# Softmax sums of the last attention unit: four key tiles summed on VectorE, two partial sums per group on TensorE

## The chip, the cores and the metric

The kernel runs on one core of one Trainium2 chip. The metric is the device time of one execution in microseconds (us), given as the median of several runs. The engines of the core have their own instruction queues and meet at semaphores: TensorE (PE in the profile, its weight loads PEld), VectorE (DVE), ScalarE (ACT), GpSimd (POOL) and SyncE (SP), whose queue issues nearly all of the transfers here.

## The reference

A decoder block on `x` of 4 x 1024 x 512 in float32: gated self-attention, cross-attention to a context of 4 x 1024 x 384, and a small feed-forward network, each behind a layer norm and added to its input. The change is in the cross-attention, which is, cut to what matters:

```python
q = (query @ Wq + bq).reshape(B, Nq, H, D).transpose(0, 2, 1, 3)    # B = 4, Nq = 1024, H = 16, D = 32
k = (key_value @ Wk + bk).reshape(B, Nkv, H, D).transpose(0, 2, 1, 3)
v = (key_value @ Wv + bv).reshape(B, Nkv, H, D).transpose(0, 2, 1, 3)
attn = jnp.einsum('bhqd,bhkd->bhqk', q, k) * scale
attn = jnp.clip(attn, -CLAMP, CLAMP)
attn = jax.nn.softmax(attn, axis=-1)
...
x = jnp.einsum('bhqk,bhkd->bqhd', attn, v).reshape(B, Nq, Cq)
return x @ Wo + bo
```

The softmax needs, for each head and query, the sum of the exponentials over all 1024 keys. How this sum is formed for the last batch element is what changes.

## The kernel before, in words

`moderate_path` does all of the work. It goes through eight **units**: `order` lists phase 0 (self-attention) and then phase 1 (cross-attention), each for the batch elements 0 to 3. The last unit, number 7, is the cross-attention of batch element 3. A unit has two halves of 512 queries (`hf`), a half has four **groups** of four heads (`g`), and a group has eight **key tiles** of 128 keys (`kt`). One call of `step(g, kt)` (L684) handles one key tile of one group, so that a unit has 64 steps.

The order of instructions is written out by hand; the instructions of each engine run in the order in which the code issues them. One step issues, in this order:

1. what `after(...)` has put on the list as due and not "behind" (`issue_due(False)`): the divisions of earlier groups;
2. `scores`: TensorE multiplies keys and queries into two PSUM tiles `s` (i = 0 for heads 0 and 1 of the group, i = 1 for heads 2 and 3; tag `s` has two buffers, L570), ScalarE takes the exponential of each into a tile `e` of 128 x 1024 (six buffers, L578 and L579), and VectorE adds `e` to running sums `es` (L585 for the first two key tiles, L587 after that);
3. what is due and "behind" (`issue_due(True)`): the closing sums of the group before (`add_up`);
4. `finish` of the step before: `times` multiplies the exponentials by the values into `av` (L601), and after the last key tile `normalize` copies `av` (L618) and has `add_up` come one step later.

Beside the steps, `run` (L933) spreads other work over them, the "items": projections (L87), layer norm, its transposes, the hidden units of the feed-forward network (ScalarE L862, VectorE L868). In the last unit these are, in each half: rest of the hidden units of an earlier half, the output projection of the half before (L87, L770, L774, L775), the feed-forward output (L879, L885), the layer norm with its way through memory (`root` L290 to L299, `norm` L303, the writing `away` L307, the reading `back` L312, the 32 x 32 block transposes L318), the input of the feed-forward network (`inputs`, L841) and then hidden units again.

**The sums before.** In units 4 to 6 (`shared` is false) VectorE adds all four heads, 14 additions of 128 x 1024 in a group, and `add_up` sums over the 128 partitions with four TensorE products with a column of ones (L631). In the last unit `shared` is true: VectorE adds only heads 0 and 1 (seven additions in a group). For heads 2 and 3 TensorE multiplies each `e` by the ones itself: at every second key tile `times` issues four such products, two key tiles by two heads (L609). `normalize` then copies that result too (L620), `add_up` issues two products for heads 0 and 1 (L631) and copies them (L632), and four small transfers bring both parts into one tile, in which `divide` adds them (L637, L642, L643, L647, L655). `divide` takes the reciprocal (L668), writes it to memory (L671) and reads it back spread over the partitions (L675); `multiply` uses it (L681).

The very last group, (unit 7, second half, group 3), is `closing`: it already has all four heads added on VectorE, and its final sums are taken by `settle` (L705) at the end, with ones repeated 32 times so that the result stands on all rows at once (L713). The code after the units (from L1045 on) finishes it: `divide` of `settle` in four pieces (L719, L720), the last projection, layer norm, transposes and feed-forward network.

All working tiles in SBUF come from pools with a fixed number of buffers for each tag. The transposed keys have the tag `k` with two buffers (L455); the last unit's keys are in one of them, and no unit after it needs the other.

Of the kernel before, what the change touches and what calls it, by code (L numbers as in the profile page):

```python
# [10 lines left out]
F32 = mybir.dt.float32  # L11
U32 = mybir.dt.uint32
AF = mybir.ActivationFunctionType
ALU = mybir.AluOpType
AX = mybir.AxisListType

P = 128
B, T, D = 4, 1024, 512
H, DH = 16, 32
NPR = H // 2  # L20
HG = 4
NT = T // P
NC = D // P
# [40 lines left out]
def moderate_path(tc: tile.TileContext, a: dict, out: bass.AP, flag: bass.AP):  # L64
    nc = tc.nc
    x = a["x"]
    with ExitStack() as st:
# [8 lines left out]
        p2 = enter(tc.tile_pool(name="mp2", bufs=2))  # L76
# [29 lines left out]
        ones = const.tile([P, 1], F32, name="ones")  # L106
# [158 lines left out]
        sm = pa.tile([P, HALF], F32, tag="sm", name="sm")  # L265
# [70 lines left out]
        order = [(ph, b) for ph in range(2) for b in range(B)]  # L336
# [5 lines left out]
        def after(steps, f, behind=False):  # L342

            soon.append((tick[0] + steps, behind, f))
# [206 lines left out]
        def attention(u, hf):  # L551

            ph, b = order[u]
            me = S[u]
            steps = []
            sums = 2 if ph == 0 else 1

            shared = ph == 0 or u + 1 == len(order)

            def apart(g):  # L560
                return 2 if u + 1 < len(order) else 3

            def closing(g):
                return (u, hf, g) == (len(order) - 1, 1, HG - 1)

            def scores(g, kt):
                q, k = me["q", hf], me["k"]
                es = []
                for i in range(2):
                    s = ps.tile([P, 2, HALF], F32, tag="s", name="s")  # L570
                    for j in range(2):
                        r = slice((2 * i + j) * DH, (2 * i + j + 1) * DH)
                        for m in range(0, P, 64):
                            nc.tensor.matmul(  # L574
                                s[m : m + 64, j, :], lhsT=k[r, g, kt * P + m : kt * P + m + 64], rhs=q[r, g, :],
                                start=True, stop=True,
                            )
                    e = p4.tile([P, 2, HALF], F32, tag="e", name="e", bufs=6)  # L578
                    nc.scalar.activation(e, s, AF.Exp, scale=SCALE)  # L579
                    es.append(e)  # L580
                me["e", kt] = es
                for i in range(1 if shared and not closing(g) else 2):
                    if kt == 1:
                        me.setdefault("es", {})[i] = p1.tile([P, 2, HALF], F32, tag=f"es{i}", name="es")
                        nc.vector.tensor_tensor(me["es"][i], me["e", 0][i], es[i], ALU.add)  # L585
                    elif kt > 1:
                        nc.vector.tensor_tensor(me["es"][i], me["es"][i], es[i], ALU.add)  # L587
                if ph == 0 and kt > 0:
                    if kt == 1:
                        me["eg"] = p1.tile([P, 2, HALF], F32, tag="es1", name="eg")  # L590
                    for h in range(2):
                        eg, gate = me["eg"][:, h, :], lambda t: me["sw"][:, t, HG * g + h, 1:2]
                        if kt == 1:
                            nc.vector.tensor_scalar(eg, me["e", 0][0][:, h, :], gate(0), None, ALU.mult)
                        nc.vector.scalar_tensor_tensor(eg, es[0][:, h, :], gate(kt), eg, ALU.mult, ALU.add)  # L595
                return es

            def times(g, kt, es):
                for h in range(HG):
                    r = slice(h * DH, (h + 1) * DH)  # L600
                    nc.tensor.matmul(  # L601
                        av[r, :], lhsT=me["v"][:, kt, HG * g + h, :], rhs=es[h // 2][:, h % 2, :],
                        start=(kt == 0), stop=(kt == NT - 1),
                    )
                if shared and kt % 2 and not closing(g):

                    for j in range(4):
                        t, h = kt - 1 + j // 2, j % 2
                        nc.tensor.matmul(  # L609
                            sm[j * DH : j * DH + sums, :],  # L610
                            lhsT=me["sw"][:, t, HG * g + 2 + h, :] if ph == 0 else ones, rhs=me["e", t][1][:, h, :],
                            start=(kt == 1), stop=(kt == NT - 1),
                        )

            def normalize(g):
                i = (u * 2 + hf) * HG + g
                both = p1.tile([P, 3, HALF], F32, tag="both", name="both")
                nc.scalar.copy(both[:, 0, :], av)  # L618
                if shared:
                    nc.scalar.copy(both[:, 1, :], sm)  # L620
                    added = [me["es"][0][:, 0, :], me["es"][0][:, 1, :]]
                    if ph == 0:
                        added += [me["eg"][:, 0, :], me["eg"][:, 1, :]]
                else:
                    added = [me["es"][h // 2][:, h % 2, :] for h in range(HG)]
                after(1, lambda: add_up(g, i, both, added), behind=True)

            def add_up(g, i, both, added):

                for j, e in enumerate(added):  # L630
                    nc.tensor.matmul(sm[j * DH : j * DH + 1, :], lhsT=ones, rhs=e, start=True, stop=True)  # L631
                nc.scalar.copy(both[:, 2, :], sm)  # L632

                c, s1, s2 = cs_[i % 2], sum1_d[i % 4], sum2_d[i % 4]
                rows = both.rearrange("(j r) s q -> j r s q", r=DH)
                n = len(added)
                nc.sync.dma_start(s1[0:n], rows[0:n, 0, 2, :])  # L637
                if not shared:
                    nc.sync.dma_start(c[:, 0, 0, :], s1[0:n].rearrange("h (q e) -> (h q) e", e=INNER))
                else:  # L640
                    for k in range(sums):
                        nc.sync.dma_start(s2[k], rows[:, k, 1, :])  # L642
                    nc.sync.dma_start(  # L643
                        c[0:64, 0:sums, 0, :], s1[0:n].rearrange("(s h) (q e) -> (h q) s e", h=2, e=INNER)
                    )
                    for k in range(sums):
                        nc.sync.dma_start(  # L647
                            c[64:, k, :, :], s2[k].rearrange("(p h) (q e) -> (h q) p e", h=2, e=INNER)
                        )
                after(apart(g), lambda: divide(g, i, both, c))  # L650
# [44 lines left out]
            def finish(g, kt, es):  # L695
                times(g, kt, es)
                if kt == NT - 1 and not closing(g):
                    normalize(g)
# [6 lines left out]
        def settle(u, hf, g):  # L705

            me = S[u]
            i = (u * 2 + hf) * HG + g
            rec = p1.tile([P, HALF], F32, tag="recb", name="recb")

            def sums():
                for j in range(HG):
                    nc.tensor.matmul(  # L713
                        sm[j * DH : (j + 1) * DH, :], lhsT=ones.to_broadcast([P, DH]), rhs=me["es"][j // 2][:, j % 2, :],
                        start=True, stop=True,
                    )

            def divide(t):
                nc.vector.reciprocal(rec[:, ts(t, P)], sm[:, ts(t, P)])  # L719
                nc.vector.tensor_tensor(me["q", hf][:, g, ts(t, P)], av[:, ts(t, P)], rec[:, ts(t, P)], ALU.mult)  # L720

            def look():
                nc.vector.tensor_reduce(marks[:, i : i + 1], sm, AX.X, ALU.add)
                nc.vector.tensor_reduce(marks[:, NS + i : NS + i + 1], rec, AX.X, ALU.add)

            return sums, divide, look
# [225 lines left out]
        def one(f):  # L952
            return [[(0, f)]]
# [4 lines left out]
        def ahead(u, what):  # L958

            return one(lambda: pres[u]["load"](what))  # L960
# [62 lines left out]
        p = pres[0]  # L1023
# [8 lines left out]
        first = p["x"][0] + one(warm) + p["ln"][0] + p["x"][1] + one(load_gates) + ahead(0, "q") + ahead(0, "v")  # L1032
# [7 lines left out]
        for u in range(n):  # L1040
            if u == 0:
                crossing.append(True)
            for hf in range(2):
                run(attention(u, hf), beside(u, hf))
# [9 lines left out]
        h = [part for item in held[0]["h"] for part in item]  # L1054
# [18 lines left out]
        h = sum(tail["h"], [])  # L1073
# [650 lines left out]
```

## Time and profile before

| what | value |
|---|---|
| time, median of 3 runs | 2200.52 us (2198.43 to 2201.12) |
| the profiled execution, first to last instruction | 2198.2 us |
| mean granted TensorE clock of that execution | 0.997 |
| first scores of the last unit | 1927.81 us after the start |
| first scores of the last unit's second half | 2036.25 us |
| last key tile's scores | 2141.55 us |
| from there to the end | 56.7 us |
| VectorE busy in all, additions L587 among it | 1562.5 us, 642.2 us |
| ScalarE busy in all, exponentials L579 among it | 1237.6 us, 993.4 us |

Times in the profile count from the first instruction of the profiled execution. "Line engine op out<-in xcount | busy us, mean ns" is a group of instructions that come from one line. The count is of the hardware's records: in float32 a product has two. The granted clock is the share of full speed at which the TensorE array was allowed to run. The chain of waits follows back from the last instruction, at each step to what released it; "idle before, releaser" is the engine's idle time and what ended it.

The work of each engine in the last unit, by stretches (the columns are: stretch, its length, then busy time and count of PE, PEld, DVE, ACT and POOL, the granted clock, the DMA engines' share and GB/s):

```profile
1927.81:1954.20 26.39, 26.15 (x260) 5.71 (x256) 14.37 (x21) 21.31 (x28) 0.00 (x0) 1.00 0.06 13
1954.20:1980.14 25.94, 25.94 (x273) 6.40 (x269) 14.55 (x27) 16.61 (x22) 0.00 (x0) 1.00 0.06 13
1980.14:2014.10 33.96, 33.70 (x328) 7.52 (x328) 25.61 (x47) 23.45 (x26) 0.19 (x1) 1.00 0.39 103
2014.10:2054.30 40.20, 39.60 (x404) 8.84 (x398) 19.94 (x33) 33.16 (x46) 0.00 (x0) 1.00 0.30 94
2054.30:2089.50 35.20, 35.20 (x357) 8.62 (x357) 17.09 (x26) 19.18 (x23) 0.00 (x0) 1.00 0.04 11
2089.50:2124.20 34.70, 34.33 (x332) 7.58 (x328) 25.61 (x46) 23.92 (x27) 0.19 (x1) 1.00 0.46 131
```

The first line is the first group of the unit; the third and the sixth are the stretches with the layer norm and its transposes, up to the input product of the feed-forward network (L841).

### The profile page before, as it was taken

To read this page: it belongs to the slowest core of one execution; us is meant where nothing else is said; L and a number is where in the kernel's file an instruction comes from. 1 tells how busy PE (TensorE), PEld (TensorE's weight loads), DVE (VectorE), ACT (ScalarE), POOL (GpSimd) and SP (SyncE) were. 2 spreads that over 40 slices of the span, in tenths; PEclk is the share of its full clock that TensorE was granted. 3 is DMA by queue.
4 is the path that set the end of the run, shared out by engine and by line. 5 is a ranking of instruction groups with operands and counts; after the bars stand their busy time and mean duration, and the time that the engine had idled before them with its cause. 6 is when DMAs were issued, how large, how long until landed. Compare 5 with 4: busy or idle time off the path is not lost.

```text
span 2198.2 us, 52765 instructions
## 1 busy us (share of the span) xinstructions
PE 2170.0 (99%) x22606; PEld 551.7 (25%) x22606; DVE 1562.5 (71%) x2526; ACT 1237.6 (56%) x1489; POOL 82.2 (4%) x118
## 2 busy tenths in 40 slices
PE   8999999999999999999999999999999999999996
PEld 3322222222222222222222222222222222222223
DVE  4478675796757957567677676877777777856477
ACT  0155545555455554555656566675757666577673
POOL 1000000030210000000000000000000000000000
PEclk9999999999999999999999999999999999999998
DMA  4412123132231221211222132222234142213131
GB/s 141 131 61 55 63 96 106 29 88 66 97 104 31 82 69 47 68 57 42 70 85 90 45 89 69 79 70 59 69 84 112 46 107 69 61 39 80 59 89 41
DMA packets 153304, 161.70 MB, mean 74 GB/s; under 512 B 46202, under 2 KB 91898, under 8 KB 151908
## 3 DMA queue, kind: packets, MB, share of 16 engines
q1 hardware_dynamic: 149068, 156.14, 24.6%
q8 instruction: 179, 2.93, 0.6%
q0 software_dynamic: 2144, 0.98, 0.3%
q10 hardware_dynamic: 1848, 1.12, 0.2%
q14 instruction: 65, 0.53, 0.1%
HBM read 115.40 MB, written 42.74 MB: 72 GB/s over the span
## 4 chain that ended last, share of the span: by engine, by line
PE 93%; DVE 3%; DMA 1%; ACT 1%; issue 1%; SPq 0%; DVEq 0%; ACTq 0%
PE f L87 36%; PE s L574 25%; PE av L601 21%; PE sm L609 6%; PE sm L631 3%; ACT e L579 1%; DMA w<-in_attn_Wo 1%; PE f L841 1%; PE f L879 1%; DVE g L868 1%; DVE es L587 1%; DMA rows_d<-r 0%; PE s L879 0%; PE f L471 0%; DMA rec_d<-rec 0%
## 5 line engine op out<-in xcount | busy, mean ns | idle before, releaser
L579 ACT ACTIVATE e<-s 128x1024 f32<-128x1024 f32 x1024 | 993.4, 1022 | 709.9 <-PE s L574 512.9
L587 DVE TENSOR_TENSOR es<-es,e 128x1024 f32<-128x1024 f32 x534 | 642.2, 1227 | 253.6 <-ACT e L579 251.6
L574 PE MATMUL s<-q,k 32*64 32x512 f32 x8192 | 607.5, 613 | 2.2 <-ACT e L579 0.5
L601 PE MATMUL av<-e,v 128*32 128x512 f32 x4096 | 550.4, 603 | 0.0
L87 PE MATMUL f<-xT,w 128*32 128x512 f32 x2816 | 333.7, 592 | 0.6 <-PE f L87 0.6
L595 DVE SCALAR_TENSOR_TENSOR eg<-e,sw,eg 128x512 f32<-128x512 f32 x448 | 318.5, 746 | 2.3
L585 DVE TENSOR_TENSOR es<-e 128x1024 f32<-128x1024 f32 x89 | 106.7, 1223 | 216.4 <-ACT e L579 185.4
L574 PEld LDWEIGHTS s<-q,k 32*64 32x64 f32 x8192 | 132.9, 130 | 445.6 <-ACT e L579 242.2
L87 PE MATMUL f<-w,q 128*32 128x512 f32 x1984 | 240.3, 593 | 0.0
L601 PEld LDWEIGHTS av<-e,v 128*32 128x32 f32 x4096 | 88.2, 108 | 403.7 <-issue 401.2
L87 PEld LDWEIGHTS f<-xT,w 128*32 128x32 f32 x2816 | 92.3, 110 | 211.0 <-issue 204.2
L609 PE MATMUL sm<-e,sw 128*2 128x512 f32 x1024 | 133.3, 592 | 0.0
L87 PE MATMUL f<-w,xT 128*32 128x512 f32 x896 | 106.0, 592 | 0.6 <-DVE q L284 0.6
L87 PEld LDWEIGHTS f<-w,q 128*32 128x32 f32 x1984 | 65.8, 110 | 148.9 <-issue 141.5
L87 PE MATMUL f<-w,ctxT 128*32 128x512 f32 x768 | 92.6, 592 | 0.0
L87 PE MATMUL f<-ctxT,w 128*32 128x512 f32 x768 | 92.3, 592 | 0.0
L862 ACT ACTIVATE hid<-sT,units 128x256 f32<-128x256 f32 x128 | 76.5, 605 | 27.9 <-DVE g L868 23.8
L778 POOL TENSOR_TENSOR r<-res,bo_bc 128x512 f32<-128x512 f32 x32 | 40.9, 1278 | 1040.7 <-DVE res L770 795.0
L868 DVE SCALAR_TENSOR_TENSOR g<-hid,units,g 128x256 f32<-128x256 f32 x120 | 57.5, 479 | 14.2 <-ACT hid L862 8.7
L631 PE MATMUL sm<-es,ones 128*1 128x512 f32 x348 | 65.0, 591 | 0.0
L770 DVE TENSOR_TENSOR res<-f,res 128x512 f32<-128x512 f32 x62 | 42.5, 685 | 18.5 <-PE f L87 9.9
L681 DVE TENSOR_TENSOR q<-both,recb 128x512 f32<-128x512 f32 x63 | 43.2, 685 | 7.0 <-DMA recb<-rec_d 7.0
(260 smaller groups left out, 1040.2 us busy)
## 6 DMA issues: line engine op xcount, KB each, us to landing
recb<-rec_d SPq DMA_DIRECT2D x252, 64.0 KB
xT<-rows_d SPq DMA_DIRECT2D x60, 256.0 KB
rows_d<-r SPq DMA_DIRECT2D x60, 256.0 KB
w<-in_xattn_Wo SPq DMA_DIRECT2D x9, 1024.0 KB
w<-wout_d SPq DMA_DIRECT2D x8, 1024.0 KB
res<-in_x SPq DMA_DIRECT2D x32, 256.0 KB
x1b_d<-r SPq DMA_DIRECT2D x32, 256.0 KB
res<-x1b_d SPq DMA_DIRECT2D x32, 256.0 KB
```

The lines of the kernel that those rows point to most:

```text
L87: nc.tensor.matmul(to[r], lhsT=lhsT[:, j, :] if len(lhsT.shape) == 3 else lhsT[:, r], rhs=rhs, **flags)
L574: nc.tensor.matmul(s[m : m + 64, j, :], lhsT=k[r, g, kt * P + m : kt * P + m + 64], rhs=q[r, g, :], start=True, stop=True,)
L579: nc.scalar.activation(e, s, AF.Exp, scale=SCALE)
L585: nc.vector.tensor_tensor(me["es"][i], me["e", 0][i], es[i], ALU.add)
L587: nc.vector.tensor_tensor(me["es"][i], me["es"][i], es[i], ALU.add)
L595: nc.vector.scalar_tensor_tensor(eg, es[0][:, h, :], gate(kt), eg, ALU.mult, ALU.add)
L601: nc.tensor.matmul(av[r, :], lhsT=me["v"][:, kt, HG * g + h, :], rhs=es[h // 2][:, h % 2, :], start=(kt == 0), stop=(kt == NT - 1),)
L609: nc.tensor.matmul(sm[j * DH : j * DH + sums, :], lhsT=me["sw"][:, t, HG * g + 2 + h, :] if ph == 0 else ones, rhs=me["e", t][1][:, h, :], ...
L631: nc.tensor.matmul(sm[j * DH : j * DH + 1, :], lhsT=ones, rhs=e, start=True, stop=True)
L681: nc.vector.tensor_tensor(me["q", hf][:, g, :], both[:, 0, :], all_, ALU.mult)
L862: nc.scalar.activation(hid, res["s"], AF.Relu, bias=units[:, 1, h : h + 1], scale=units[:, 0, h : h + 1])
L868: nc.vector.scalar_tensor_tensor(res["g"], res["hid"], units[:, 2, h - 1 : h], res["g"], ALU.mult, ALU.add)
```

## The change

Only the last unit changes; `shared` is now phase 0 alone, and the last unit is called `fours`. It takes the unused buffer of the tag `k` and cuts it into four tiles of 128 x 2 x 512, two sets of two. At each key tile VectorE adds `e` of all four heads (i = 0 and 1) to the set of the current four key tiles: key tiles 0 to 3 go into the first set, 4 to 7 into the second. The key tiles 0 and 4 have no addition of their own, since the next one adds the two directly. That makes 12 additions in a group instead of seven. After key tile 3, the new function `by_ones` sums the first set over the partitions with four TensorE products that begin the accumulation in `sm`; it is issued two steps later, behind that step's scores. `add_up`, as before one step after `normalize`, adds four products for the second set to the same accumulation. The products L609 at every second key tile, the copy L620, one write and one read of the small transfers and the addition in `divide` are gone in the last unit.

In the closing group the additions of the key tile 7 are left out. Its first set is summed during the group with the 32-fold ones (`by_ones` at key tile 5), and at the end `sums` issues four products for the second set and four for the two tiles `e` of key tile 7 directly.

```diff
-            shared = ph == 0 or u + 1 == len(order)
+            shared = ph == 0
+            fours = u + 1 == len(order)
+            if fours and "sets" not in me:
+                spare_k = p2.tile([P, NC, T], F32, tag="k", name="sets")
+                me["sets"] = [spare_k[:, i, :].rearrange("p (a t) -> p a t", a=2) for i in range(NC)]
...
                 me["e", kt] = es
-                for i in range(1 if shared and not closing(g) else 2):
+                if fours:
+                    if kt == 4 * (kt // 4) or closing(g) and kt == NT - 1:
+                        return es
+                    to = me["es"] = me["sets"][2 * (kt // 4) : 2 * (kt // 4) + 2]
+                    for i in range(2):
+                        nc.vector.tensor_tensor(to[i], me["e", kt - 1][i] if kt % 4 == 1 else to[i], es[i], ALU.add)
+                    if kt == 3:
+                        after(2, lambda: by_ones(g, to, True, False), behind=True)
+                    return es
+                for i in range(1 if shared else 2):
...
+            def by_ones(g, tiles, first, last):
+                width = DH if closing(g) else 1
+                for j in range(HG):
+                    nc.tensor.matmul(
+                        sm[j * DH : j * DH + width, :], lhsT=ones.to_broadcast([P, width]) if width > 1 else ones,
+                        rhs=tiles[j // 2][:, j % 2, :], start=first, stop=last,
+                    )
+
+            me["by ones"] = by_ones
...
-                if shared and kt % 2 and not closing(g):
+                if shared and kt % 2:
...
                 for j, e in enumerate(added):
-                    nc.tensor.matmul(sm[j * DH : j * DH + 1, :], lhsT=ones, rhs=e, start=True, stop=True)
+                    nc.tensor.matmul(sm[j * DH : j * DH + 1, :], lhsT=ones, rhs=e, start=not fours, stop=True)
...
             def sums():
-                for j in range(HG):
-                    nc.tensor.matmul(
-                        sm[j * DH : (j + 1) * DH, :], lhsT=ones.to_broadcast([P, DH]), rhs=me["es"][j // 2][:, j % 2, :],
-                        start=True, stop=True,
-                    )
+                me["by ones"](g, me["es"], False, False)
+                me["by ones"](g, me["e", NT - 1], False, True)
```

More of the change, by code (lines that the diff above doesn't have):

```diff
@@ L610, in times @@
                             sm[j * DH : j * DH + sums, :],
-                            lhsT=me["sw"][:, t, HG * g + 2 + h, :] if ph == 0 else ones, rhs=me["e", t][1][:, h, :],
+                            lhsT=me["sw"][:, t, HG * g + 2 + h, :], rhs=me["e", t][1][:, h, :],
                             start=(kt == 1), stop=(kt == NT - 1),
@@ L620, in normalize @@
                     nc.scalar.copy(both[:, 1, :], sm)
-                    added = [me["es"][0][:, 0, :], me["es"][0][:, 1, :]]
-                    if ph == 0:
-                        added += [me["eg"][:, 0, :], me["eg"][:, 1, :]]
+                    added = [me["es"][0][:, 0, :], me["es"][0][:, 1, :], me["eg"][:, 0, :], me["eg"][:, 1, :]]
                 else:
```

## The prediction

> **What bounds the kernel.** I read the page first, then the groups of the last unit by line, the chain of waits there, TensorE's timeline step by step, and stretches of the clock.
>
> ```profile
> span 2198.2 us, 52765 instructions
> PE 2170.0 (99%) x22606; PEld 551.7 (25%) x22606; DVE 1562.5 (71%) x2526; ACT 1237.6 (56%) x1489; POOL 82.2 (4%) x118
> PE 93%; DVE 3%; DMA 1%; ACT 1%; issue 1%; SPq 0%; DVEq 0%; ACTq 0%
> ```
>
> TensorE is the bound of the whole, so its work is what counts; but a busy share of 99% hides waits inside a product's modelled span, and in the last unit the others come close. The groups of that unit, from its first scores to the end of its additions:
>
> ```profile
> L587 DVE TENSOR_TENSOR es<-es,e 128x1024 f32<-128x1024 f32 x56 | 67.9, 1223 | 43.4 <-ACT e L579 42.9
> L609 PE MATMUL sm<-e,ones 128*1 128x512 f32 x224 | 29.2, 592 | 0.0
> L631 PE MATMUL sm<-es,ones 128*1 128x512 f32 x36 | 8.2, 591 | 0.0
> ```
>
> VectorE's additions wait for exponentials, so it has room on average. The 224 records of L609 are what TensorE loses. Their price stands in the chain through steps without items:
>
> ```profile
> 2022.06 1.06 PE s L574 x16
> ...
> 2023.14 1.03 ACT e L579
> ...
> 2024.22 2.00 PE s L574 x16
> 2026.22 1.00 PE av L601 x8
> 2027.22 0.86 PE sm L609 x8
> 2028.08 1.06 PE s L574 x16
> ```
>
> Eight records of ones, four products side by side, take 0.86 us. The scores take 1.06 us when both their PSUM buffers are free, and 2.00 us when the second is still read: then its half waits for the second exponential. So short and long steps alternate.
>
> **The rule of a step without items**, from these rows. Scores start at 0; exponentials end at about 2.17 and 3.15 (first one 1.15 after its scores start, 1.02 long, the second 0.95 behind). TensorE is done with scores and values at 2.1; the first buffer is free at 2.22, so the next step starts there, has scores of 2.00 us, then values, 2.94 in all, or 3.80 with a block of sums. By then both buffers are free again. A pair is thus 2.22 + 3.80 = 6.02 with sums and 5.16 without. TensorE's timeline shows both: steps of 2.23 and 3.79 in the third and fourth group, and 2.30 and 2.86 in the closing group, which has no L609.
>
> **The change, part by part.** Removed for each of seven groups: four blocks of L609 at 0.86 us, and a pair L631 that lengthens the step by 0.82 (4.58 against 3.76). Added: two blocks of 0.86, the size that the four L631 products of unit 6's last group show (issued from 1931.97, the values behind them from 1932.83). Net per group 3.44 + 0.82 - 1.72 = 2.54 of TensorE work, 17.8 for seven. The closing group pays one block inside and one at its end, 1.72 more. Net 16.1 us of work; what reaches the end depends on each stretch.
>
> - *First group* (1927.81 to 1954.20, 26.39 us). With the rule its steps become 2.23, 3.76, 2.22, 2.94, 2.22, 3.80, 3.84, 3.76 (the last two carry 1.72 us of projection): 24.77, **-1.6**.
> - *Second group* up to the step at 1980.14. Each step carries 1.72 us of projection and TensorE never waits: three sum blocks go, one comes, the add-up stays (4.61 for 4.58): **-1.7**. VectorE has ten additions at 1.17 (four in a row take 4.63), three times 1.57 for L770, L774, L775, and some nine L868 at 0.48: 21 of 24 us, so it just holds.
> - *Fourth group of the first half and first group of the second* (2015.97 to 2054.30, 38.33 us): pairs of 5.16, and the two added blocks fall in long steps: 36.5, **-1.8**. The check on the cover: per group VectorE has 14.0 us of additions and about 5 of L868, L681 and L668 in 22.4 us. It lags by at most two steps, and `e` has three steps of buffers. ScalarE has 16 exponentials at 0.95, eight hidden units and two copies at about 0.5: 20.2 of 22.4.
> - *Second group of the second half* (2054.30 to 2089.50, 35.20 us): TensorE-bound. Four sum blocks go, one comes, and its first step loses the 0.9 us wait inside its scores, as the alternation is out of step with before: 31.9, **-3.3**.
> - *The two third groups.* TensorE alone would come to the feed-forward input product L841 at 30.7 us after the step that begins the stretch (1980.14 and 2089.50), against 34 and 34.7. It can't use that: L841 stands in its queue behind a chain of VectorE and transfers:
>
> ```profile
> 2112.76 5.55 DMA rec_d<-rec
> ...
> 2119.61 1.97 DMA recb<-rec_d
> ...
> 2121.70 0.06 DVE q L681
> ...
> 2122.31 1.22 DVE es L587
> 2123.53 0.63 DVE xn L318
> ...
> 2124.20 1.91 PE f L841 x27
> ```
>
>  The last transpose (L318) is behind the addition of key tile 7, and that behind L681, which waits for the reciprocals to come back. After the change that one addition is two. Earlier on VectorE the additions of key tiles 6 and 7 delay L303 by about 1.3 us. SP gives that back: L307's second pair now waits behind L643 and L647 (2105.38 to 2106.59, its data ready at 2105.29), and two of those four transfers go. The extra additions of key tiles 1 to 6 fill idle time (1.7, 0.4, 0.9 and 1.6 us before additions, L318 and L681), helped by key tile 4's, which goes. So L841 comes 1.17 later in each stretch, with TensorE idle 4.6 and 5.2 us before it: **+1.2 twice**. Bounds for one: -3.4 (chain as short as TensorE's own time) to +5.9 (all five extra additions in it).
> - *Closing group*: one block more in a pair that keeps its alternation, between 0 and 0.86; I take **+0.5**.
> - *The end*: VectorE's last two additions (to 2148.00) and the hidden units behind them now hold L719 until 2150.11. Without the additions L719 waits for the sums, 16 records from 2147.71, 1.72 and some drain: about 2149.65, **-0.45** of the 2.35 that VectorE saves.
> - ScalarE's copies L620 (seven at 0.60) and L655 lie beside TensorE: nothing, and if ScalarE bound its steps, 4 us. The spare key buffer was last read by unit 6's scores, so no wait.
>
> These make -5.95.
>
> **The clock.** Long idle time of TensorE is new inside the units, and at the end the trace shows its price:
>
> ```profile
> 2163.36:2166.77 3.41, 1.92 (x16) 0.85 (x16) 3.03 (x14) 1.05 (x2) 0.35 (x1) 1.00 0.00 0
> 2166.77:2170.18 3.41, 1.27 (x40) 1.06 (x44) 2.78 (x9) 2.40 (x4) 0.00 (x0) 1.00 0.00 0
> 2170.18:2173.59 3.41, 3.41 (x36) 2.01 (x30) 0.55 (x2) 0.58 (x1) 0.00 (x0) 0.50 0.03 7
> ```
>
> (stretch, length, PE, PEld, DVE, ACT and POOL busy, granted clock.) After 3.41 us with TensorE busy for 1.27 the clock was 0.50 for the next 3.41; after 1.92 busy it stayed at 1.00. A gap of 4.6 or 5.2 us leaves over 2 us idle in at least one such stretch however they fall, so each should be followed by up to 3.41 us at half speed, at most 1.7 us lost. Part may fall in the gap itself: 1.45 each, **+2.9**. The lower bound is 0, the upper 3.4 for both.
>
> The Trainium skill, "TensorE: Matmul & The Clock Gate", Part 1, speaks against the change in the same place but is milder: it halves the clock after an idle window of about 3.4 us, on a window that runs freely. By its words a gap of 4.6 us need not hold a whole window. Two gaps with whole windows in them would make the sum -2.55, none -5.95.
>
> **Sum.** -5.95 + 2.9 = -3.05. The profiled execution was 2198.25, which would become 2195.2; the median of the runs was 2200.52, 0.1% above it, and becomes **2197.5**.
>
> **Rivals.**
>
> 1. *The gain comes through without the clock's price, or with shorter chains.* For it: VectorE idles 6 us of each third-group stretch, and the first stretch's gap of 4.6 us is short. Without the clock term 2194.5; with the chains also as short as before 2192.2; TensorE's whole 16.1 would be 2184.4, which the alternation of steps speaks against. Faster by over 0.2%. Chance 0.37.
> 2. *VectorE becomes the bound in the third groups: slower.* If L303 is late enough that the reading `back` moves with it, all five extra additions stand in front of L841: 5.85 instead of 1.17 in both halves, 9.4 more, and with the same clock loss 2206.9; half of that, 2202.2. It decides from about 2 us of delay at L307's second pair in each half, which uses up what SP gives back; beyond 3.8 us per half the change loses over 0.2%. For it: VectorE was busy 25.6 of 34 us there and gets 6 more. Against it: the gaps named above lie between the additions. Chance 0.14.
> 3. *It does not shorten what it removes*: in the stretches without items the pair stays at 6 us since exponentials, not sums, set it. Then the -1.6 and -1.8 go, 2200.9, no change. Against it the closing group's 5.16. Chance 0.05.
>
> The forecast has 0.44, with its own range 2195 to 2200. About 0.2%, or 4.4 us, is what a measurement of this kernel tells from no change. Faster than 2196.1: rival 1 and a little of the forecast, 0.40; within 0.2%: 0.46; slower: 0.14. The range 2190.5 to 2202 takes in the clock's and the chains' bounds on the side of gain, and half of rival 2.
>
> **What would show it.** Steps of 2.2 and 2.9 where there were 2.2 and 3.8 without items; 3.76 where there was 4.62 with projections; TensorE idle 4 to 6 us before L841 in both halves, ended by L318, and a clock of 0.50 after it; L719 about 0.45 earlier against the last scores. Wrong would be: no such gap (the change is then worth 6 us or more), or gaps over 7 us or hidden units waiting for VectorE between them (it then loses).

## The result, and the profile after

The changed kernel takes 2201.95 us (median of 13 runs, 2195.4 to 2203.93) against 2200.37 us for the kernel before (13 runs, 2197.45 to 2201.83). The ratio is 1.0004, with a 95% interval of 0.9997 to 1.0012: no change that can be told. The profiled execution of the changed kernel took 2200.93 us with a span of 2199.07.

The head of its page and the line of the chain by engine:

```profile
span 2199.1 us, 52499 instructions
PE 2162.2 (98%) x22482; PEld 545.9 (25%) x22482; DVE 1594.5 (73%) x2550; ACT 1233.7 (56%) x1482; POOL 81.7 (4%) x118
PE 92%; DVE 4%; issue 1%; DMA 1%; ACT 1%; SPq 0%; DVEq 0%; ACTq 0%
```

TensorE has 7.8 us less busy time and VectorE 32 us more, and the span is the same: TensorE now waits. The groups of the last unit, from its first scores to the closing sums (the changed kernel's lines are numbered higher: L591 are the additions into the sets, L614 is `by_ones`, L652 `add_up`, L859 the input product that was L841):

```profile
L591 DVE TENSOR_TENSOR sets<-sets,e 128x1024 f32<-128x1024 f32 x62 | 73.1, 1221 | 9.3 <-ACT e L583 9.2
...
L591 DVE TENSOR_TENSOR sets<-e 128x1024 f32<-128x1024 f32 x32 | 37.8, 1221 | 30.6 <-ACT e L583 30.6
...
L614 PE MATMUL sm<-sets,ones 128*1 128x512 f32 (+1 forms) x66 | 9.8, 592 | 0.0
...
L859 PE MATMUL f<-xn,win 128*32 128x256 f32 x64 | 8.2, 592 | 8.4 <-DVE xn L318 8.4
...
L652 PE MATMUL sm<-sets,ones 128*1 128x512 f32 x56 | 7.3, 590 | 0.0
```

The 224 records of L609 are gone, 94 additions stand where there were 63 (seven groups of seven and 14 in the closing one), and one group has an idle time that it did not have: L859 waits 8.4 us for VectorE's transposes L318. TensorE's timeline around the first of the two waits (start, length, line, count, idle time before and its releaser):

```profile
2004.15 2.00 PE L578 MATMUL s<-q,k 32*64 32x512 f32 x16
2006.08 1.06 PE L624 MATMUL av<-e,v 128*32 128x512 f32 x8
2007.08 1.31 PE L578 MATMUL s<-q,k 32*64 32x512 f32 x16
2008.31 1.07 PE L624 MATMUL av<-e,v 128*32 128x512 f32 x8
2009.20 0.60 PE L859 MATMUL f<-xn,win 128*32 128x256 f32 x4
2013.14 3.51 PE L859 MATMUL f<-xn,win 128*32 128x256 f32 x28 [3.35 <-DVE xn L318]
2016.59 1.11 PE L578 MATMUL s<-q,k 32*64 32x512 f32 x16
```

A step without sums takes 2.93 us (2004.15 to 2007.08), as the rule in the prediction had it. Then TensorE idles for 3.35 us, and L859, for which the kernel before took 1.91 us with all its 32 records, takes 3.51 us for 28. The stretches of the clock say why (stretch, length, busy time of PE, PEld, DVE, ACT and POOL, granted clock, DMA share, GB/s):

```profile
2009.57:2012.99 3.42, 0.23 (x4) 0.00 (x0) 3.42 (x4) 1.25 (x2) 0.00 (x0) 1.00 0.00 0
2012.99:2016.40 3.41, 3.25 (x28) 1.36 (x28) 0.10 (x1) 0.00 (x0) 0.00 (x0) 0.50 0.00 0
2016.40:2019.81 3.41, 3.41 (x42) 0.88 (x48) 1.01 (x1) 3.04 (x5) 0.00 (x0) 1.00 0.00 0
```

TensorE was busy for 0.23 of 3.42 us, and for the next 3.41 us its clock was 0.50. The second half is the same with a longer wait, 5.01 us:

```profile
2118.81:2122.22 3.41, 0.00 (x0) 0.00 (x0) 3.37 (x4) 0.59 (x1) 0.00 (x0) 1.00 0.00 0
2122.22:2125.63 3.41, 3.14 (x28) 1.33 (x28) 0.21 (x1) 0.00 (x0) 0.00 (x0) 0.50 0.00 0
```

This is its chain:

```profile
2109.02 5.66 DMA rec_d<-rec
...
2115.98 2.79 DMA recb<-rec_d
...
2118.85 0.06 DVE q L702
...
2119.46 2.35 DVE sets L591 x2
2121.81 0.63 DVE xn L318
...
2122.49 3.45 PE f L859 x28
```

It has the order of the chain before, reciprocals back, L702 (L681 before), addition, last transpose, with two additions where there was one, 2.35 us for 1.22.

By stretches of the last unit, cut at the starts of TensorE's steps (us; the kernel before and the changed one):

| stretch (steps) | before | changed | difference | forecast |
|---|---|---|---|---|
| up to the unit | 1927.81 | 1928.18 | +0.37 | 0 |
| first group (0 to 8) | 26.40 | 25.33 | -1.07 | -1.6 |
| second group (8 to 14) | 25.93 | 24.20 | -1.73 | -1.7 |
| third group with L841 (14 to 25) | 35.83 | 38.87 | +3.04 | +1.2 and 1.45 |
| to the second half's first group (25 to 38) | 38.33 | 36.32 | -2.01 | -1.8 |
| second group (38 to 46) | 35.19 | 31.72 | -3.47 | -3.3 |
| third group with L841 (46 to 57) | 36.56 | 41.25 | +4.69 | +1.2 and 1.45 |
| closing group (57 to 63) | 15.49 | 16.28 | +0.79 | +0.5 |
| end | 56.70 | 56.92 | +0.22 | -0.45 |

So 8.3 us were won in four stretches, as forecast, and 7.7 us of it were given back in the two stretches with L841. The records of L841 that wait for the last transpose start 35.43 and 37.87 us after the start of their stretch, in the kernel before 34.21 and 34.71: 4.4 us of the 7.7 are this later start. The other 3.3 us lie between that start and the next scores (3.44 and 3.38 us, before 1.62 and 1.85), at half the clock.

### The profile page after: what moved, and what is told of

Read it like the earlier page. It is cut to its first block, busy times and chain, and to the rows that moved or that the text cites. A ratio compares the mean times of both kernels' runs of the same rounds, so it can differ in the third digit from the quotient of the medians.

```text
span 2199.1 us, 52499 instructions
## 1 busy us (share of the span) xinstructions
PE 2162.2 (98%) x22482; PEld 545.9 (25%) x22482; DVE 1594.5 (73%) x2550; ACT 1233.7 (56%) x1482; POOL 81.7 (4%) x118
## 4 chain that ended last, share of the span: by engine, by line
PE 92%; DVE 4%; issue 1%; DMA 1%; ACT 1%; SPq 0%; DVEq 0%; ACTq 0%
PE f L87 36%; PE s L578 25%; PE av L624 21%; PE sm L632 5%; PE sm L652 3%; DVE sets L591 1%; PE f L859 1%; ACT e L583 1%; DMA rec_d<-rec 0%; PE f L897 0%; DVE g L886 0%; PE sm L614 0%; DVE res L903 0%; PE f L471 0%; DMA recb<-rec_d 0%
## 5 line engine op out<-in xcount | busy, mean ns | idle before, releaser
L600 DVE TENSOR_TENSOR es<-es,e 128x1024 f32<-128x1024 f32 x480 | 576.8, 1228 | 211.3 <-ACT e L583 209.6
L624 PE MATMUL av<-e,v 128*32 128x512 f32 x4096 | 544.8, 603 | 0.0
L598 DVE TENSOR_TENSOR es<-e 128x1024 f32<-128x1024 f32 x80 | 95.8, 1223 | 192.9 <-ACT e L583 166.3
L591 DVE TENSOR_TENSOR sets<-sets,e 128x1024 f32<-128x1024 f32 x62 | 73.1, 1221 | 9.3 <-ACT e L583 9.2
L886 DVE SCALAR_TENSOR_TENSOR g<-hid,units,g 128x256 f32<-128x256 f32 x120 | 57.6, 480 | 12.9 <-ACT hid L880 7.7
L591 DVE TENSOR_TENSOR sets<-e 128x1024 f32<-128x1024 f32 x32 | 37.8, 1221 | 30.6 <-ACT e L583 30.6
L652 PE MATMUL sm<-es,ones 128*1 128x512 f32 x320 | 57.8, 591 | 0.0
```

Of the source, the lines that this page charges most:

```text
L591: nc.vector.tensor_tensor(to[i], me["e", kt - 1][i] if kt % 4 == 1 else to[i], es[i], ALU.add)
L624: nc.tensor.matmul(av[r, :], lhsT=me["v"][:, kt, HG * g + h, :], rhs=es[h // 2][:, h % 2, :], start=(kt == 0), stop=(kt == NT - 1),)
L886: nc.vector.scalar_tensor_tensor(res["g"], res["hid"], units[:, 2, h - 1 : h], res["g"], ALU.mult, ALU.add)
```

## The experiments

Two theories were to be told apart. **Theory 1**: TensorE's product L841 waits in its queue for a chain of VectorE and transfers that two additions lengthen, and the gap then halves the clock. **Theory 2**: VectorE is simply full in the third groups, so that only less work for it would help. Ratios are to the kernel before, on the same chip.

**The transposes together, ahead of L681 and of the additions.**

```diff
-                out += weave(last["tr"], pause(3)) + last["s"] + weave(some(last, 8), pause(14))
+                out += last["tr"] + pause(3) + last["s"] + weave(some(last, 8), pause(14))
```

> The changed kernel with the four block transposes L318 of the last unit issued together, ahead of L681 and of the additions of key tile 7; nothing else moves. Theory 1 (L841 stands in TensorE's queue behind a chain that ends with the reciprocals' return, L681, two additions and the last transpose, and the clock halves after the gap): L841 starts when the read of the rows has landed and four transposes are done, about 5.3 us earlier in the second half and 4.1 us in the first, the clock stays at 1.00 there (1.7 us each), together some 12 us less than the changed kernel, about 2190 us. Theory 2 (VectorE is simply full in the third groups): the order of its work does not matter, at most 2 us, 2200 to 2202.

Measured: 2189.33 us (5 runs), ratio 0.9959 [0.9946, 0.9973]. The profile has no half clock before 2158.74 us, 28 us behind the last scores. VectorE in the first half:

```profile
2006.39 2.48 DVE L318 STREAM_TRANSPOSE xn<-xn 128x512 f32<-128x512 f32 x4
2009.77 0.69 DVE L702 TENSOR_TENSOR q<-both,recb 128x512 f32<-128x512 f32 x1 [0.91 <-DMA recb<-rec_d]
2010.38 2.35 DVE L591 TENSOR_TENSOR sets<-sets,e 128x1024 f32<-128x1024 f32 x2
```

The fourth transpose is done at 2008.87, ahead of L702's wait, and L841 starts 31.7 us after the start of the stretch (35.4 in the changed kernel), 32.8 in the second half (37.9). TensorE itself comes to L841 31.47 us after the start, so in the first half next to nothing is left of the wait. No work of VectorE was removed, so theory 2 falls: it was the order.

The same move on the kernel before:

> The kernel before with the same move of the transposes. Theory 1: TensorE itself reaches L841 34 us after the start of the stretch, where it had waited 0.7 us in the second half alone; so 0 to -1 us, 2199.5 to 2200.5. Theory 2: nothing, 2200.4. If it gains as much as it does on the changed kernel, the change to the sums has no part in it.

Measured: 2199.23 us (10 runs), 0.9997 [0.9988, 1.0007]. The third group of the second half goes from 36.56 to 35.83 us, the rest is unchanged. The move is worth something only with the changed sums, since with the sums as before TensorE itself reaches L841 only 34.0 us after the start of the stretch; without the move the last transpose ends at 33.9 and 34.7 us, so at most 0.7 us is to be won.

**The gap filled with idle products.**

```diff
                 ss = res["ss"]
+                if (u, hf) in ((n - 2, 1), (n - 1, 0)):
+                    for i in range(4):
+                        nc.tensor.matmul(ss, lhsT=ident, rhs=bo_bc, start=True, stop=True)
```

> The changed kernel with four idle products of 128 x 512 on TensorE just ahead of L841 in both halves of the last unit, overwritten by L841 itself. Theory 1: they fill 3.4 us of gaps of 4.6 to 7 us, the clock stays at 1.00 after them, L841 takes 1.7 us and not 3.4: about 3.4 us less than the changed kernel, 2198.5 us, and a smaller spread between runs. Rival (the chain of VectorE alone costs, the clock's halving is hidden behind ScalarE or does not depend on the gap): no change, 2202 us.

Measured: 2195.18 us (11 runs, 2193.3 to 2197.43), 0.9983 [0.9974, 0.9992]. TensorE's timeline in the first half (L858 are the idle products, L862 is L841):

```profile
2008.84 3.70 PE L858 MATMUL f<-bo_bc,ident 128*128 128x512 f32 x8
2012.47 1.93 PE L862 MATMUL f<-xn,win 128*32 128x256 f32 x32
2014.33 1.11 PE L578 MATMUL s<-q,k 32*64 32x512 f32 x16
```

More work on TensorE made the kernel faster. In the first half L841 begins 35.46 us after the start of the stretch, as in the changed kernel (35.43), and takes 1.93 us; the stretch shrinks from 38.87 to 37.08. With L841 starting at the same point, the 1.79 us are the price of the half clock. That the starts agree is chance: in this execution the reciprocals came back at least 1.3 us earlier and the last transpose ended 34.04 us after the start (35.37 in the changed kernel), and L841 then waited for the idle products, which ended at 35.29. In the second half L841 also came 2.0 us earlier (35.85 for 37.87), which the products do not explain; there L681 found its reciprocals 2.1 us earlier than in the changed kernel's profile, with the same order of instructions. The whole fell by 6.8 us, more than the 3.4 us expected; the clock in the two halves is worth 3.4 to 3.6 of it, the rest is not shown to come from the filling.

The runs of the changed kernel without the filling fit this: its 13 times go roughly with the mean granted clock of each run, 2195.4 and 2195.7 us at 0.997, 2203.2 to 2203.9 us at 0.994. With the filling the runs lie within 4.1 us, not 8.5; those of the kernel before lie within 4.4.

**Key tile 7 of the third groups summed directly** (the two additions removed from the chain, a block on TensorE added behind L841):

```diff
-                    if kt == 4 * (kt // 4) or closing(g) and kt == NT - 1:
+                    if kt == 4 * (kt // 4) or (closing(g) or g == 2) and kt == NT - 1:
...
+                direct = fours and g == 2
                 for j, e in enumerate(added):
-                    nc.tensor.matmul(sm[j * DH : j * DH + 1, :], lhsT=ones, rhs=e, start=not fours, stop=True)
+                    nc.tensor.matmul(sm[j * DH : j * DH + 1, :], lhsT=ones, rhs=e, start=not fours, stop=not direct)
+                if direct:
+                    by_ones(g, me["e", NT - 1], False, True)
```

> The changed kernel without the additions of key tile 7 in the two third groups; TensorE sums those two tiles itself in the add-up (one block of 0.86 us more, behind L841). Theory 1: two additions leave the chain to L841, 2.35 us each, less 0.86 us each: about -3 us, 2199 us. Rival (L841 waits for the transfers, VectorE's additions beside them are hidden): +1.7 us, 2203.5 us.

Measured: 2192.47 us (6 runs), 0.9966 [0.9954, 0.9978]. The sign is theory 1's, the size was missed, 9.5 us under the changed kernel where 3 were expected: L841 came 3.6 and 4.6 us earlier (31.8 and 33.3), not 2.35, as in this execution the reciprocals also came back 1.3 and 2.3 us earlier; and with the shorter gaps no half clock followed, which the expectation had left out.

**L681 of the second group two steps later**, the additions and the transposes as in the changed kernel:

```diff
-                after(apart(g), lambda: multiply(g, both, all_), behind=u + 1 < len(order))
+                after(apart(g) + 2 * (fours and g == 1), lambda: multiply(g, both, all_), behind=u + 1 < len(order))
```

> The changed kernel with L681 of the second group issued two steps later, so that the additions of key tile 7 and the last transpose of the third group no longer stand behind the reciprocals' return; the transposes stay where they were. Theory 1: L841 starts two additions and a transpose after the third transpose, about 33.6 us after the start of the stretch in the first half (35.4 in the changed kernel) and about 35 in the second (37.9), in the second without the scatter of the transfers; 2 to 5 us less than the changed kernel, more where a half-speed stretch goes with it. Rival (the additions, not the return, set L841): no change in the first half.

Measured: 2192.88 us (6 runs), 0.9968 [0.9956, 0.998]. L841 started at 33.5 and 34.8 us. This removes only the wait for the transfer; two additions and a transpose are what is left of the chain, and L841 came where the expectation had it. TensorE idled 1.42 and 1.68 us before it and no half clock followed. The whole is 9.1 us under the changed kernel, more than the 2 to 5 expected, but the two half clocks (1.79 us each by the filling) are part of that.

**The third groups summed as before** (L609 for heads 2 and 3 there, the rest as changed):

```diff
+            asbefore = lambda g: ph == 0 or fours and g == 2
...
-                if fours:
+                if fours and g != 2:
...
-                if shared and kt % 2:
+                if asbefore(g) and kt % 2:
```

> The changed kernel with the third group of both halves summed as in the kernel before (heads 0 and 1 on VectorE, heads 2 and 3 by L609 on TensorE). Theory 1: one addition, not two, behind L681, and TensorE reaches L841 some 1.7 us sooner than before: gap of 2 to 3 us, no or little half clock; the other groups' gain of about 7 us comes through, 2194 to 2196. Theory 2 (the change gains nothing in the other groups either): 2199 to 2200.

Measured: 2193.81 us (8 runs), 0.9972 [0.9962, 0.9982]. The four winning stretches are as in the changed kernel to 0.02 us, and the third groups take 36.95 and 37.52 us, about 1 more than before. The first L303 starts 12.19 us after the start of the first stretch, 10.89 before: the extra additions of the second group's key tiles 6 and 7 stand ahead of it. TensorE idled 0.67 and 1.31 us before L841, less than the 2 to 3 expected. No half clock followed.

**The closing group's change alone, on the kernel before:**

```diff
+                if closing(g):
+                    if kt == 4 * (kt // 4) or kt == NT - 1:
+                        return es
...
+                me["by ones"](g, me["es"], False, False)
+                me["by ones"](g, me["e", NT - 1], False, True)
```

> The kernel before with the change in the closing group alone: two sets, the first summed at key tile 5, key tile 7 summed directly at the end. Theory: one block more in a long step, +0.8 us, and L719 no earlier since TensorE's sums end when VectorE used to be done: +0.5 to +1 us over the kernel before. Rival (the forecast's -0.45 at the end, the block half hidden): 0.

Measured: 2201.11 us (11 runs), 1.0005 [0.9996, 1.0015]. The runs can't tell it from 0. The steps can: the closing group takes 16.26 us for 15.49, and L719 begins 8.62 us after the last scores, in the kernel before 8.56.

**The closing sums ahead of the projection**, with the transposes together:

```diff
-        go(o[0])
-        sums()
+        sums()
+        go(o[0])
```

> The changed kernel with the four transposes ahead, and at the end the closing group's sums issued on TensorE ahead of the first three quarters of the output projection (24 records, 2.58 us), not behind them. Theory (the end gained nothing because L719 moved from waiting for VectorE to waiting for TensorE, where the sums are twice as many and stand behind the projection): L719 starts 2.3 to 2.6 us earlier against the last scores, about 6.2 us after them where it was 8.6, and the whole is some 2 us under the transposes' move alone, 2187. Rival (VectorE's hidden units still hold L719): nothing, 2189.

Measured: 2187.50 us (5 runs), 0.9944 [0.993, 0.9957]. L719 begins 6.04 us after the last scores. The chain of the changed kernel there (L614 are the closing sums, L737 is L719):

```profile
2146.43 2.15 PE f L87 x20
2148.57 0.42 PE sm L614 x2
...
2149.00 1.29 PE sm L614 x12
2150.29 0.42 PE f L87 x2
2150.71 0.04 PE sm L614 x2
...
2150.77 0.97 DVE recb L737
```

and with the sums first:

```profile
2135.89 1.29 PE sm L614 x11
2137.18 0.42 PE f L87
...
2137.61 6.03 PE f L87 x52
...
2143.66 0.70 DVE res L788
```

In the changed kernel VectorE, which had been the last to be ready, waits for sums that stand behind the projection; with the sums first the projection itself (6.03 us) is what the residual addition waits for. The gain at the end was partly lost before it in this profile: the second step of the fourth group took 5.10 us, not 2.96 as with the transposes alone. The chain there goes through the late reciprocals, L681 (L702 here), the additions of key tile 7 behind it, and TensorE's closing sums of the third group (L652), which need those additions:

```profile
2110.01 3.29 DMA recb<-rec_d
...
2113.38 0.06 DVE q L702
...
2113.99 2.37 DVE sets L591 x2
...
2116.39 0.60 PE sm L652 x2
```

ScalarE was late there as well: the step's exponentials stand behind L618 (L641 here), which copies `av` into the one buffer of `both`; it started at 2114.15 after 1.87 us of idle time, right behind the end of L681 (2113.38 to 2114.07), the last reader of that buffer. (The view names L859 as what ended this idle time, but that had been over for 1 us.)

**L841 one step later**, on top of that:

```diff
-                out += last["tr"] + pause(3) + last["s"] + weave(some(last, 8), pause(14))
+                out += last["tr"] + pause(5) + last["s"] + weave(some(last, 8), pause(12))
```

> As the run before, and L841 one step later in both halves (two pauses more ahead of it, two fewer behind). Theory: what is left of the gap before L841 (1.0 and 2.1 us with the transposes ahead) is filled by a step's work; up to -3 us, 2184 to 2186. Rival: the hidden units behind L841 come a step later and push the end; 2187 or more.

Measured: 2189.57 us (5 runs), 0.9951 [0.9937, 0.9965]. The expectation was wrong: the stretches with L841 became 1.7 and 1.5 us shorter, but the stretch behind the first one took 39.41 us for 36.32, since L841 and the hidden units moved into it.

**All three moves together** (transposes, sums first, L681 later):

> Transposes ahead, the closing sums ahead of the projection, and L681 of the second group two steps later. Theory: the wait of 2.1 us in the second step of the fourth group, where exponentials wait for VectorE's additions behind L681, goes; 2185.5 to 2187 and less scatter. Rival (that wait was one execution's): as with the first two moves, 2187.5.

Measured: 2187.20 us (5 runs, 2186.62 to 2188.47), 0.9945 [0.9931, 0.9958]. In the time this can't be told from the first two moves alone. The additions of key tile 7 now stand ahead of L681, and the closing sums no longer wait for them. What is left, and what the expectation had left out, is the copy L618: it starts at 2115.45, right behind the end of L681 at 2115.36, and L681 two steps later does not release it sooner. The step took 3.47 us in this profile, with reciprocals that came back at another time, so whether the third move is worth anything stays open. Both versions are some 0.55% faster than the kernel before.

## Why the prediction was right or wrong

The time, 2201.95 us, lies in the range, and the case with the largest chance, no change that can be told, is what came. The forecast of 2197.5 was 4.5 us low; the profiled span, at 2199.07 for a forecast of 2195.2, 3.9 us. Its mechanism is what the profile shows: a gain in four stretches, given back at L841 through a longer chain and the clock. Half of the 3.9 us is one term, the second stretch with L841 (4.69 us for 2.65); the end has 0.7, the first group 0.5, the first stretch with L841 0.4, the closing group 0.3 (0.79 for 0.5), and the start of the unit 0.4. That gain and loss cancel to within a microsecond or two is luck: no part of the reasoning makes them equal, and the runs of the changed kernel go from 2195.4 to 2203.9.

- **The rule of a step** held. Steps of 2.23 and 2.93 us replaced 2.23 and 3.79, and 3.76 replaced 4.62; the stretches of the second group and of the fourth came within 0.25 us. Rival 3 falls with that.
- **First group**: -1.07, not -1.6. Its eighth step took 4.44 us and not 3.76: a hidden unit on ScalarE waited 2.08 us for VectorE's L886 (L868 before), which stood behind two additions and L681, and the exponentials behind it came late. The same kind of loss, not in the forecast, stands in the last step of the second groups (3.84 and 3.78 us for 3.10): VectorE was said to "just hold", but bursts of two additions make others late. In these last steps TensorE's feed-forward product waits for a bank that L903 empties, and L903 is behind two additions:

```profile
1979.99 2.36 DVE L591 TENSOR_TENSOR sets<-sets,e 128x1024 f32<-128x1024 f32 x2 [0.35 <-ACT e L583]
...
1982.27 1.28 DVE L903 TENSOR_TENSOR res<-f,res 128x512 f32<-128x512 f32 x2
...
1983.01 0.29 PEld L897 LDWEIGHTS f<-wout,g 64*128 64x128 f32 x2 [0.91 <-DVE res L903]
```

- **The chain to L841.** In the first half the term was right in size: L841 came 1.22 us later in its stretch, for a forecast of 1.17. (The chain itself ended 1.51 us later, 35.37 for 33.86; before, L841 had stood behind TensorE's own work for 0.35 us more.) TensorE came to L841 at 31.5 us, not 30.7, by the last step of the second group, so its gap was 3.35 us, less than the 4 to 6 that were to show the mechanism. In the second half L841 came 3.16 us later, and the gap was 5.01 us. The term was mis-sized there because it took the transfers' times from one execution: the way from the write of the reciprocals to L681 took 9.8 us (24.40 to 34.23 after the start of the stretch) in the changed kernel's profile, 8.9 before, and the reading of the rows, ahead of that write in the queue, began 1.2 us later. The last writing of the rows (L307) was issued only 0.2 us later than before, so SyncE did give the delay back as forecast, but it took some 1 us longer to land. With the same order in the filled version it was 8.6 us, and L841 came at 35.85, where the forecast of 34.7 and 1.17 puts it.
- **The clock.** Forecast at 1.45 us for each gap; measured in the filled version, with L841 starting at the same point, 1.79. It came in both halves. The Trainium skill, "TensorE: Matmul & The Clock Gate", Part 1, asks for an idle window of about 3.4 us. The second gap held one, with TensorE busy for 0.00 us. The first gap's stretch of 3.42 us had TensorE busy for 0.23, and half speed followed there too, as the rows of before say.
- **The end.** The forecast's -0.45 was +0.06 at L719. It reckoned 1.72 us for the 16 records of the closing sums, and they took 2.3, from 2148.39 to 2150.71. The rest of the end's +0.22 is not settled: in the profile the half clock lasted 6.83 us near 2170, before 3.41, and that differs from run to run.
- **Rival 2**, all the added work in the chain, did not come; the second half's loss is of the size of half of it, but the profile shows transfers and clock there. **Rival 1** did not come as such, but the runs of the changed kernel near 2195.5 us at a clock of 0.997 may be what it described; no trace of one was kept.

What stays open is why the transfers of the second half differ by 1 to 2 us between executions.

## What to carry to other kernels

Work taken from the busiest engine is won only up to the next product in its queue that waits for someone else; look for that product first, and move what it waits for ahead in the other engine's queue together with the change. Here the change alone was worth nothing, and the move of the transposes alone nothing, but the two together 0.4%. An idle gap of 3 to 5 us on TensorE cost more than its length here, 1.8 us at half the clock, and filling it with useless products gave that back.

## What the runs showed of the hardware

The first is the clock: it halves well before a stretch is wholly idle. The stretches have a length of 3.41 us and a phase that differs from run to run. In all the profiles here, from the last unit's start to 2180 us, full-speed stretches in which TensorE was busy for up to 1.44 us were followed by half speed and those with 1.73 us or more were not. A stretch that was at half speed itself was followed by another with TensorE busy for up to 2.80 us, and by full speed from 2.91 us on: at half the clock, an estimated 1.40 and 1.46 us of work at full speed, so much the same limit. Between 1.44 and 1.73 us it went both ways; the closing-only version and the one with the sums first, a stretch and the one after it:

```profile
2168.06:2171.47 3.41, 1.53 (x49) 1.32 (x53) 2.75 (x8) 2.40 (x4) 0.00 (x0) 1.00 0.00 0
2171.47:2174.89 3.42, 3.42 (x42) 1.60 (x35) 2.07 (x4) 0.58 (x1) 0.00 (x0) 1.00 0.05 16
```

```profile
2163.37:2166.78 3.41, 1.55 (x12) 0.79 (x10) 3.06 (x8) 2.52 (x5) 0.00 (x0) 1.00 0.59 218
2166.78:2170.19 3.41, 3.41 (x7) 0.91 (x6) 2.84 (x8) 3.41 (x7) 0.00 (x0) 0.50 0.01 2
```

So a gap of some 4 us may cost nothing or 1.8 us, by where it falls. Two gaps make 3.6 of the 8.5 us over which the changed kernel's runs spread; the transfers' differing times may be part of the rest, but no trace of its fastest or slowest run was kept.

The second is the small write of the reciprocals. It took 5.66 us when issued behind the reading of the rows (four transfers of 256 KB), where the same write early in the unit, with no such transfers ahead, took 1.4 us before (issued at 1937.82, its reader at 1939.23). The Trainium skill, "DMA: Bandwidth & Descriptors", in its section on queues, rings and completion order, says that a transfer's semaphore lands only after every earlier write of its DMA engine. The trace agrees: the transposes that waited for the reading started at 2114.63, and the small write landed at 2114.68. It can't tell this from a plain wait in the queue behind the reading, with the DMA engines busy for 0.93 of that time.
